# Multiplying the experts' low-rank factors on four partition groups, from a DRAM copy laid out for it

## The chip, the cores and the metric

The kernel runs on one core of one Trainium2 chip. The core has a matrix engine (TensorE, PE in the profile), a vector engine (VectorE, DVE), a scalar engine (ScalarE, ACT), GpSimd (POOL) and SyncE (SP), which in this kernel issues most of the transfers between DRAM and the on-chip memory SBUF. Matmuls write to PSUM, from where DVE or ACT read. The engines run side by side, each its own instructions in order, and wait for each other by semaphores. The metric is the time of one execution on the device in microseconds (us); several executions are made and the median is given. One further execution is recorded by the hardware profiler, and the trace and the profile page come from that one.

## The reference

Two transformer layers over `x` of 4 x 1024 tokens with 256 features, all in fp32. Layer 0 is causal attention and a feed-forward block beside each other, layer 1 is gated group attention and a mixture of eight experts of which each token uses two. What the change touches are the weights of the experts: each is a dense matrix and a product of two low-rank factors (rank 16).

```python
# layer 0
xn = layernorm(x)
x = x + attention0(xn) + relu(xn @ W1 + b1) @ W2 + b2
# layer 1, experts (E = 8, D = 256, HID = 512, R = 16)
def _lora_in(xf, W, b, A, B):                   # W [E, HID, D], A [E, R, D], B [E, HID, R]
    base = einsum('td,ehd->teh', xf, W)
    low = einsum('ter,ehr->teh', einsum('td,erd->ter', xf, A), B)
    return base + low + b
...
h1 = _lora_in(xf, W1, b1, A1, B1)
h3 = _lora_in(xf, W3, b3, A3, B3)
g = silu(h1) * h3
y_e = _lora_out(g, W2, b2, A2, B2)              # the same with HID and D exchanged
y = einsum('te,ted->td', gates, y_e)            # gates: top 2 of 8, normalised
```

Since `base + low` is `xf` times (W + A B), the kernel adds the products A B to the dense weights once, and uses the sum for all tokens.

## The kernel before

Layer 0 is a loop over 16 **units** `u` of 256 tokens: batch `b = u // 4`, quarter `p = u % 4`. The tokens' rows stay in SBUF (`xs`). The source gives each unit's steps in a fixed sequence, interleaved with steps of its neighbours; within that, the framework's scheduler puts the instructions of each engine into an order when the program is built, by what it estimates to be ready, and from then on each engine's order is fixed. In unit `u` stand, in the source:

- `turns` (L549 to L557): the attention weights of unit `u` are transposed on PE (`pt`, L554) and copied to `attT`, for half 0 by ACT, for half 1 by DVE (L556).
- `hidden` (L534 to L546): the feed-forward block, PE L541 and ReLU on ACT L544.
- `first_turn(u + 2)`: a normalised unit is transposed, from unit 3 on by a DVE transpose of a strip read back from DRAM (L457).
- `merge(u, qTs[u])`: the loads for the merging of expert weights; described below.
- `queries(u + 1)`, then `norms_turn(u - 1)` (L632 to L646): the layer-1 input `xl` of the unit before is transposed on PE (L638) and copied by ACT.
- `weighted(u)` (L560 to L580): attention weights times values. For units with `p > 0` from unit 2 on, distant weights come back from DRAM as two bands, which DVE transposes (L568) into `attT`; PE L573 and L576; DVE forms `zT`.
- `logits(u - 1)` (PE L655), `scores(u + 1)`, the second half of `hidden`, statistics of a later unit.
- `finish(u)` (L584 to L606): PE `po` (L592) and `pv` (L596); ACT squares `pv` and forms `rs` (L601, L190, L191); DVE adds into `x` (L598, L605) and takes statistics (L184 and L185).
- `multiply()`: the products that `merge` returned (in the last unit ahead of `finish`).
- `norms(u)` (L609 to L631): from the statistics a chain DVE, ACT (logarithm and exponential at L190 and L191), DVE (L615, L616), ACT again, DVE (L618, L620), then `xl` (L623, two instructions), ACT `xr` (L627).

The merging shares 8 experts out over the 16 units: unit `u` does half `c = u % 2` of expert `e = u // 2`. With `c == 0` the expert's six factors, one packed row of 3 x 768 for each rank, are loaded by three transfers to `lt` [96, 768] at partitions 0, 32 and 64, 16 partitions each (L400). One buffer serves for `lt`, so the loads for the next expert wait for the last multiplication from it. Each unit loads 768 KB of dense weights to `wt` (L405). `multiply` makes three products of 128 x 512 in PSUM, the third from two matmuls, adds each to `wt` on DVE (L419), and stores the sums to the DRAM tensors `wm13` and `wm2` (L420, L422), which the expert stage of layer 1 reads.

`second` (L334 to L358) is called at unit 0 and puts layer 1's weights and constants on SP's queue: `raw`, `rowt`, `wvl_s`, `wg_s`, `wo_s`, `rope_s`, then zeros to `yg`, `posb_s`, and the bias columns and rows of the experts (`cols`, eight of `eb2`). The loads of the first `merge` follow on the same queue. A DMA of SP is issued under one of eight semaphores in turn, and waits for the transfer that used it last.

Of the kernel before, what the change touches and what calls it, by code (L numbers as in the profile page):

```python
# [9 lines left out]
F32 = mybir.dt.float32  # L10
AF = mybir.ActivationFunctionType
ALU = mybir.AluOpType
# [5 lines left out]
P = 128  # L18
B, N, D = 4, 1024, 256
NT = N // P  # L20
DC = D // P
# [4 lines left out]
E, HID, R = 8, 512, 16  # L26
# [21 lines left out]
EB2, W2B = EC * D, EC * D + D  # L48

LN_ = D + HID  # L50

# [14 lines left out]
def block_kernel(ctx: ExitStack, tc: tile.TileContext, x, wq, wk, wv, wfc, w1, w2, wqk, wvl, wg,  # L68
                 wo, wr, ew, el, eb2, cols, rows, rope, posb, out):
    nc = tc.nc  # L70
# [15 lines left out]
    def load_x(b, p, n=1, after=None):  # L86
        tt = slice(2 * p, 2 * (p + n))
        w = nc.sync.dma_start(out=xs[b][:, tt, :], in_=x[b].rearrange("(t p) d -> p t d", p=P)[:, tt, :])
        if after is not None:
            tc.add_manual_dep(w.ins, after.name, landed, reason="what is needed first goes first")  # L90
# [80 lines left out]
    dram = ctx.enter_context(tc.tile_pool(name="dram", bufs=1, space=DRAM))  # L171
# [5 lines left out]
    atd = dram.tile([B * NP, 2 * P, (NP - 1) * 2 * P], F32, name="atd")  # L177

    rd = [dram.tile([N, 4 * QK], F32, name=f"rd{b}") for b in range(B)]
    xld = [dram.tile([P, DC, N], F32, name=f"xld{b}") for b in range(B)]  # L180

    def stats(src, mv, t, tag="st"):
# [57 lines left out]
    with ExitStack() as l0:  # L240
        wp = l0.enter_context(tc.tile_pool(name="l0w", bufs=1))
        p_sc = l0.enter_context(tc.tile_pool(name="p_sc", bufs=2, space=PSUM))
# [8 lines left out]
        act = l0.enter_context(tc.tile_pool(name="l0a", bufs=2))  # L251
# [84 lines left out]
        def second(after):  # L336
            def load(eng, **k):
                tc.add_manual_dep(eng.dma_start(**k).ins, after.name, landed, reason="what is needed first goes first")

            load_x(1, 0, NP, after)  # L340
            raw = wp.tile([P, DC, QK], F32, name="raw")
            load(nc.sync, out=raw, in_=wqk)
            load(nc.sync, out=wqr_s[:, :, QK:], in_=wr)
            load(nc.sync, out=rowt, in_=rows[RE:].partition_broadcast(P))
            load(nc.sync, out=wvl_s, in_=wvl)
            load(nc.sync, out=wg_s, in_=wg)
            load(nc.sync, out=wo_s, in_=wo)
            load(nc.sync, out=rope_s, in_=rope)

            load(nc.sync, out=yg[NF * TB + NSURE * HB :, :].rearrange("(k p) d -> p k d", p=P),  # L350
                 in_=zero.unsqueeze(1).to_broadcast([P, (NHB - NSURE) * HB // P, D]))

            nc.gpsimd.memset(posb_s, FAR)
            for g in range(P // G):
                load(nc.sync, out=posb_s[ts(g, G), ts(g, G)], in_=posb)
            for name, at in (("eb1", EB1), ("eb3", EB3)):
                nb = COLS[name][0]
                load(nc.sync, out=wm13[:, :, at : at + EC].rearrange("e p m -> p e m"),  # L358
                     in_=cols[:, nb : nb + E * EC].rearrange("p (e m) -> p e m", e=E))
            for e in range(E):  # L360
                load(nc.sync, out=wm2[e, :, EB2:], in_=eb2[e].partition_broadcast(P))
            return raw
# [32 lines left out]
        def merge(u, after):  # L395
            e, c = u // DC, u % DC
            if c == 0:
                lt = act.tile([96, LN_], F32, tag="lt", name="lt", bufs=1)
                for k in range(3):
                    w = nc.sync.dma_start(out=lt[32 * k : 32 * k + R, :], in_=el[e][:, k * LN_ : (k + 1) * LN_])  # L400
                    tc.add_manual_dep(w.ins, after.name, landed, reason="what is needed first goes first")
                merge.lt = lt
            lt = merge.lt
            wt = act.tile([P, 3, HID], F32, tag="wt", name="wt")
            w = nc.sync.dma_start(out=wt, in_=ew[e].rearrange("p (k c w) -> p k c w", k=3, c=DC)[:, :, c, :])  # L405
            tc.add_manual_dep(w.ins, after.name, landed, reason="what is needed first goes first")
            f1, f3, f2 = lt[0:R, :], lt[32 : 32 + R, :], lt[64 : 64 + R, :]

            def multiply():

                pab, pc = (p_sc.tile([P, 2, HID], F32, tag="sc", name=n) for n in ("pab", "pc"))
                pa, pb, pc = pab[:, 0], pab[:, 1], pc[:, 0].rearrange("p (i d) -> p i d", i=2)
                nc.tensor.matmul(pa, f1[:, ts(c, P)], f1[:, D : D + HID], start=True, stop=True)
                nc.tensor.matmul(pb, f3[:, ts(c, P)], f3[:, D : D + HID], start=True, stop=True)
                for i in range(2):
                    nc.tensor.matmul(pc[:, i, :], f2[:, ts(2 * c + i, P)], f2[:, HID : HID + D],
                                     start=True, stop=True)
                for k, p in enumerate((pa, pb, pc.rearrange("p i d -> p (i d)"))):
                    nc.vector.tensor_tensor(wt[:, k, :], p, wt[:, k, :], ALU.add)  # L419
                nc.sync.dma_start(  # L420
                    out=wm13[e, :, 0:EB1].rearrange("p (k c w) -> p k c w", k=2, c=DC)[:, :, c, :], in_=wt[:, 0:2, :])
                nc.sync.dma_start(out=wm2[e, :, ts(c, HID)], in_=wt[:, 2, :])  # L422
            return multiply
# [310 lines left out]
        for u in range(U):  # L734
            b, p = divmod(u, NP)
# [4 lines left out]
            if u == 0:  # L740
                raw = second(qTs[0])
# [16 lines left out]
            if u == 0:  # L758
                fuse_values()
            multiply = merge(u, qTs[u])  # L760
            if u + 1 < U:
                qT = queries(u + 1)
# [677 lines left out]
```

## Time and profile before

| what | value |
|---|---|
| median of 3 runs | 1122.03 us (1120.65 to 1123.66) |
| profiled execution | 1116.86 us |
| its span, first to last instruction | 1115.2 us |
| mean granted TensorE clock | 0.997 |
| PE busy from 110 to 115 us, and from 115 to 120 us | 5.00 and 5.00 us |
| DVE busy in the same stretches | 1.47 and 4.21 us |
| adds of the merge, L419, 128x512, `pab` / `pc` | 0.666 / 0.678 us each |
| load of dense weights, L405, 16 times 768 KB | 6.0 us to landing |
| load of factors, L400, 48 KB each, the first three | 4.5 us to landing |

The profiled execution lies below all three timed runs; what is worked out from its rows is worth what it is against its own time. In rows of the trace, the first number is the start in us from the span's start, the second is the busy time of the row, which may hold several instructions (x8). "L413" is the line, then come the operation, the output and the inputs by their names in the program, and their sizes. A bracket at the end gives the idle time of the engine ahead of the row and what ended it. PE is the matmul, PEld the load of its weights, SPq the issuing of transfers on SP. An fp32 matmul leaves two records for its two passes.

### The profile page before, as it was taken

Reading aid. Unit: us, or ns where it says so; the run is one execution under the profiler, and the core shown is the slowest. Engines: PE = TensorE matmul, PEld = TensorE weight load, DVE = VectorE, ACT = ScalarE, POOL = GpSimd, SP = SyncE. Lnnn points to the kernel's source line nnn. Section 1 sums busy time; section 2 is a strip of 40 time slices with the busy share of each in tenths; the row PEclk is TensorE's granted clock in tenths of the full one; section 3 lists DMA queues with packets and bytes.
Section 4 is the critical chain, followed back from the end, with each engine's and each line's share of the span. In section 5 each row is a group of like instructions: output and inputs, shape, how many; then the busy total and the mean of one; then the engine's idle time right before and its main releaser. Section 6 shows DMA issues by size and latency. Waiting matters only on the chain. (4 is left out here: it accounts for less than half of the span.)

```text
span 1115.2 us, 15338 instructions
## 1 busy us (share of the span) xinstructions
PE 1099.2 (99%) x5084; PEld 861.1 (77%) x5084; DVE 557.0 (50%) x1536; ACT 285.4 (26%) x755; POOL 173.8 (16%) x216
## 2 busy tenths in 40 slices
PE   8999999999999999999999999999999999999997
PEld 6788888888888888874588888888888885555645
DVE  5434464445544355456674554454332323384956
ACT  3323333234333232224201111111111112112021
POOL 2200001222131113332000000000000003362410
PEclk9999999999999999999999999999999999999999
DMA  8735434564454335521547887787877764353211
GB/s 311 202 101 155 136 100 132 162 190 118 118 175 131 116 101 165 162 109 43 183 118 239 272 266 223 211 285 218 258 233 233 232 173 103 94 138 90 81 42 39
DMA packets 211953, 180.06 MB, mean 161 GB/s; under 512 B 135968, under 2 KB 181536, under 8 KB 206752
## 3 DMA queue, kind: packets, MB, share of 16 engines
q1 hardware_dynamic: 121200, 141.03, 40.0%
q10 hardware_dynamic: 84528, 21.25, 8.4%
q0 software_dynamic: 6144, 16.79, 4.6%
q8 instruction: 41, 0.67, 0.3%
q14 instruction: 40, 0.33, 0.1%
HBM read 125.93 MB, written 54.17 MB: 161 GB/s over the span
## 5 line engine op out<-in xcount | busy, mean ns | idle before, releaser
L959 PE MATMUL p<-xT,w 128*128 128x256 f32 (+1 forms) x1152 | 241.2, 368 | 0.0
L959 PEld LDWEIGHTS p<-xT,w 128*128 128x128 f32 x1152 | 209.4, 190 | 26.9 <-issue 0.3
L964 ACT ACTIVATE s<-p,w 128x256 f32<-128x256 f32 (+1 forms) x144 | 58.8, 459 | 313.9 <-PE p L959 210.4
L1044 POOL DMA_INDIRECT y<-yg,slot x64 | 61.7, 964 | 487.4 <-DVE v L1169 420.4
L968 DVE SCALAR_TENSOR_TENSOR g<-p,w,s 128x256 f32<-128x256 f32 (+1 forms) x144 | 61.0, 462 | 137.3 <-PE p L959 131.4
L981 PE MATMUL py<-w,g 128*128 128x256 f32 x544 | 123.4, 379 | 0.0
L541 PE MATMUL pm<-xnT,w_s 128*128 128x256 f32 x512 | 118.5, 379 | 0.0
L592 PE MATMUL po<-w_s,hT 128*128 128x256 f32 x512 | 116.1, 380 | 0.0
L981 PEld LDWEIGHTS py<-w,g 128*128 128x128 f32 x544 | 102.9, 190 | 14.1 <-DVE g L968 0.3
L592 PEld LDWEIGHTS po<-w_s,hT 128*128 128x128 f32 x512 | 96.9, 190 | 20.1 <-issue 8.0
L541 PEld LDWEIGHTS pm<-xnT,w_s 128*128 128x128 f32 x512 | 95.6, 192 | 11.6
L716 POOL DMA_INDIRECT xg<-xr,put x64 | 63.7, 995 | 209.2 <-ACT hT L544 138.8
L494 PE MATMUL sc<-xnT,qT 128*128 128x256 f32 (+1 forms) x320 | 65.8, 361 | 0.0
L544 ACT ACTIVATE hT<-pm,colt 128x256 f32<-128x256 f32 x128 | 53.9, 466 | 42.3 <-PE pm L541 42.2
L596 PE MATMUL pv<-vo_s,zT 128*128 128x512 f32 x128 | 60.1, 592 | 0.0
L1167 PE MATMUL pv<-wvl_s,xl 128*128 128x512 f32 x128 | 57.7, 597 | 1.6 <-DVE v L1169 1.5
L494 PEld LDWEIGHTS sc<-xnT,qT 128*128 128x128 f32 x320 | 54.6, 191 | 6.0 <-ACT qT L481 0.2
L1243 PE MATMUL pg<-xl,wg_s 128*128 128x512 f32 x128 | 58.3, 595 | 0.0
L1290 PE MATMUL pj<-wo_s,gd 128*128 128x256 f32 x256 | 56.7, 380 | 0.6 <-DVE o L1292 0.4
L1290 PEld LDWEIGHTS pj<-wo_s,gd 128*128 128x128 f32 x256 | 48.1, 190 | 7.9 <-DVE o L1292 0.9
L605 DVE SCALAR_TENSOR_TENSOR x<-pv,rs,x 128x256 f32<-128x256 f32 x32 | 15.5, 484 | 72.4 <-ACT rs L191 57.1
L983 DVE TENSOR_TENSOR yt<-py,w 128x512 f32<-128x512 f32 (+1 forms) x36 | 23.8, 660 | 51.1 <-PE py L981 51.1
(261 smaller groups left out, 1330.2 us busy)
## 6 DMA issues: line engine op xcount, KB each, us to landing
w<-wm SPq DMA_DIRECT2D x36, 1028.0 KB, 7.4
w<-wm SPq DMA_DIRECT2D x36, 640.0 KB, 4.7
wt<-in_ew_dram SPq DMA_DIRECT2D x16, 768.0 KB, 6.0
wm<-wt SPq DMA_DIRECT2D x16, 512.0 KB, 2.8
xt<-xg ACTq DMA_DIRECT2D x128, 64.0 KB, 4.3
yg<-yt ACTq DMA_DIRECT2D x32, 256.0 KB, 5.2
xnd<-xn SPq DMA_DIRECT2D x16, 256.0 KB, 3.3
wm<-wt SPq DMA_DIRECT2D x16, 256.0 KB, 2.9
```

What stands on the lines that cost most here:

```text
L494: nc.tensor.matmul(sc[:, kp * 2 * P : kp * 2 * P + w], qT[:, c, ts(i, P)], xnTs[b * NP + kp][:, c, 0:w], start=(c == 0), stop=(c == DC - 1))
L541: nc.tensor.matmul(pm[:, j, :], w1_s[:, c, ts(2 * m2 + j, P)], xnTs[u][:, c, :], start=(c == 0), stop=(c == DC - 1))
L592: nc.tensor.matmul(po[:, i, :], hT[:, m, ts(i, P)], w2_s[:, m, :], start=(m == 0), stop=(m == IC - 1))
L596: nc.tensor.matmul(pv, zT[:, c, ts(i, P)], vo_s[:, c, :, :], start=(c == 0), stop=(c == DC - 1))
L716: w = nc.gpsimd.indirect_dma_start(out=xg, out_offset=bass.IndirectOffsetOnAxis(ap=put[:, b * NT + t : b * NT + t + 1], axis=0), in_=xrs[b ...
L959: nc.tensor.matmul(p[:, j, :], w13[:, w0 : w0 + P], xT[:, c, :], start=(c == 0), stop=(c == DC - 1))
L964: up.silu = nc.scalar.activation(s[:, j, :], p1[:, j, :], AF.Silu, bias=w13[:, EB1 + m : EB1 + m + 1]).ins
L968: up.g = nc.vector.scalar_tensor_tensor(g[:, m, :], p3[:, j, :], w13[:, EB3 + m : EB3 + m + 1], s[:, j, :], ALU.add, ALU.mult).ins
L981: down.last = nc.tensor.matmul(py[:, k, :], g[:, m, ts(k, P)], w2[:, m * D : (m + 1) * D], start=(m == 0), stop=(m == EC - 1)).ins
L1044: w = nc.gpsimd.indirect_dma_start(out=ys[b][:, t, k, :], out_offset=None, in_=yg, in_offset=bass.IndirectOffsetOnAxis(ap=slot[:, n : n + ...
L1243: gate_sum.last = nc.tensor.matmul(pg, wg_s[:, c, ts(m, P)], a.xl[:, c, ts(h, T * P)], start=(c == 0), stop=(c == DC - 1)).ins
L1290: nc.tensor.matmul(pj, a.gd[:, m, ts(n, P)], wo_s[:, m, :], start=(m == 0), stop=(m == HC - 1))
```

## The change

The factors of all experts are first copied, within DRAM, to a tile `eld` of 4 groups x 128 rows (8 experts x 16 ranks) x 896 columns. Ten DMAs on SP's queue do that (five for each `k`), placed in `second` behind `rope_s` and ahead of `yg`; one of each five has pieces of 128 numbers (512 bytes). Together they write 1.57 MB.

`lt` becomes [128, 896], loaded from `eld` by four transfers at partitions 0, 32, 64 and 96 (16 x 640 for groups 0 and 1, 16 x 896 for groups 2 and 3). Groups 0 and 1 hold the first factors of `W1` and `W3` with 384 of the 512 columns (`CUT`) of the second. Groups 2 and 3 hold each a half of the factors of `W2` (256 columns of output), and beside them the first factor of `W1` or `W3` again with the last 128 columns of the second. So each group streams 384 columns in a unit. `multiply` has six matmuls instead of four, and still three adds, of 768, 512 and 256 columns (two of them on two separate stretches) instead of three times 512.

When the program is built, the scheduler orders instructions anew. On PE the merge stays where it was, behind `finish`, save that in the last unit another part of it is placed ahead of L638. On DVE, in units 1 to 13, the order from L605 on was `x`, statistics L184, add, L185, add, add, L615, L616, L618, L620, copy of `attT`, `xl`, both band transposes. It becomes `x`, add (768), L184, add (512), L185, add (256), L615, L616, copy of `attT`, L618, L620, and then, in units 1, 2, 6 and 10, one band transpose, `xl`, and the other; in unit 3 the transpose of a strip, `xl`. In unit 0 the adds come behind the first of the two `xl`. On ACT a ReLU of `hidden` is placed between the second logarithm and exponential of `norms`. On SP the ten copies stand where the source has them, and the four loads of `lt` directly behind the loads of `eb2`. The order in layer 1 is unchanged.

```diff
+CUT = HID - P
...
+    eld = dram.tile([4, E * R, 3 * D + P], F32, name="eld")
...
             load(nc.sync, out=rope_s, in_=rope)
+
+            rows_el = el.rearrange("e r n -> (e r) n")
+            for k in range(2):
+                a0 = k * LN_
+                load(nc.sync, out=eld[k, :, 0 : D + CUT], in_=rows_el[:, a0 : a0 + D + CUT])
+                load(nc.sync, out=eld[2 + k, :, 0:D].rearrange("r (c p) -> r c p", c=DC),
+                     in_=rows_el[:, 2 * LN_ : 2 * LN_ + HID].rearrange("r (c i p) -> i r c p", c=DC, i=2)[k])
+                load(nc.sync, out=eld[2 + k, :, D : 2 * D], in_=rows_el[:, 2 * LN_ + HID :])
+                load(nc.sync, out=eld[2 + k, :, 2 * D : 3 * D], in_=rows_el[:, a0 : a0 + D])
+                load(nc.sync, out=eld[2 + k, :, 3 * D :], in_=rows_el[:, a0 + D + CUT : a0 + LN_])
...
-                lt = act.tile([96, LN_], F32, tag="lt", name="lt", bufs=1)
-                for k in range(3):
-                    w = nc.sync.dma_start(out=lt[32 * k : 32 * k + R, :], in_=el[e][:, k * LN_ : (k + 1) * LN_])
+                lt = act.tile([P, 3 * D + P], F32, tag="lt", name="lt", bufs=1)
+                for k in range(4):
+                    n = D + CUT if k < 2 else 3 * D + P
+                    w = nc.sync.dma_start(out=lt[32 * k : 32 * k + R, 0:n], in_=eld[k, e * R : (e + 1) * R, 0:n])
...
-            f1, f3, f2 = lt[0:R, :], lt[32 : 32 + R, :], lt[64 : 64 + R, :]
+            f = [lt[32 * k : 32 * k + R, :] for k in range(4)]
             def multiply():
-                pab, pc = (p_sc.tile([P, 2, HID], F32, tag="sc", name=n) for n in ("pab", "pc"))
-                pa, pb, pc = pab[:, 0], pab[:, 1], pc[:, 0].rearrange("p (i d) -> p i d", i=2)
-                nc.tensor.matmul(pa, f1[:, ts(c, P)], f1[:, D : D + HID], start=True, stop=True)
-                nc.tensor.matmul(pb, f3[:, ts(c, P)], f3[:, D : D + HID], start=True, stop=True)
+                pab, pcd = (p_sc.tile([P, 2, HID], F32, tag="sc", name=n) for n in ("pab", "pcd"))
+                for k in range(2):
+                    nc.tensor.matmul(pab[:, k, 0:CUT], f[k][:, ts(c, P)], f[k][:, D : D + CUT], start=True, stop=True)
                 for i in range(2):
-                    nc.tensor.matmul(pc[:, i, :], f2[:, ts(2 * c + i, P)], f2[:, HID : HID + D],
+                    nc.tensor.matmul(pcd[:, i, 0:D], f[2 + i][:, ts(c, P)], f[2 + i][:, D : 2 * D],
                                      start=True, stop=True)
-                for k, p in enumerate((pa, pb, pc.rearrange("p i d -> p (i d)"))):
-                    nc.vector.tensor_tensor(wt[:, k, :], p, wt[:, k, :], ALU.add)
+                for k in range(2):
+                    nc.tensor.matmul(pcd[:, k, D:CUT], f[2 + k][:, 2 * D + c * P : 2 * D + (c + 1) * P],
+                                     f[2 + k][:, 3 * D :], start=True, stop=True)
+                w2 = wt[:, 2, :].rearrange("p (i d) -> p i d", i=2)
+                for out, more in ((wt[:, 0:2, 0:CUT], pab[:, :, 0:CUT]), (w2, pcd[:, :, 0:D]),
+                                  (wt[:, 0:2, CUT:], pcd[:, :, D:CUT])):
+                    nc.vector.tensor_tensor(out, more, out, ALU.add)
```

## The prediction

> **What bounds the kernel now.** I read the page from its first row, then the engines' busy time in stretches, then single rows around one merge.
>
> ```profile
> span 1115.2 us, 15338 instructions
> PE 1099.2 (99%) x5084; PEld 861.1 (77%) x5084; DVE 557.0 (50%) x1536; ACT 285.4 (26%) x755; POOL 173.8 (16%) x216
> ```
>
> TensorE has records on it 99% of the time, VectorE half. Cut into 5 us pieces, the stretch from 25 to about 475 us (where layer 0 ends) has PE busy 5.00 of 5.00 in each piece I asked for. So layer 0, which holds all that changes, is PE's: an edit counts as far as it shortens PE's queue or makes PE wait. Of unit 2 (rows of PE and DVE, others left out):
>
> ```profile
> 113.95 0.69 PE L413 MATMUL pab<-lt 16*128 16x512 f32 x1
> 113.95 0.69 PE L414 MATMUL pab<-lt 16*128 16x512 f32 x1
> 113.96 0.69 PE L416 MATMUL pc<-lt 16*128 16x256 f32 x2
> ...
> 114.48 0.59 PE L413 MATMUL pab<-lt 16*128 16x512 f32 x1
> ...
> 115.02 0.33 PE L554 MATMUL pt<-ident,att 128*128 128x128 f32 x1
> ...
> 115.13 0.48 DVE L605 SCALAR_TENSOR_TENSOR x<-pv,rs,x 128x256 f32<-128x256 f32 x1 [2.36 <-PE pc L416]
> 115.99 0.67 DVE L419 TENSOR_TENSOR wt<-pab,wt 128x512 f32<-128x512 f32 x1
> 116.58 0.17 DVE L185 BATCH_NORM_AGGREGATE mean<-st 128x2 f32<-128x6 f32 x1
> 119.26 0.73 DVE L623 TENSOR_SCALAR xl<-x,mean,rstd 128x256 f32<-128x256 f32 x2
> 119.90 1.83 DVE L568 STREAM_TRANSPOSE attT<-band 128x768 f32<-128x768 f32 x2
> ...
> 120.59 0.60 PE L638 MATMUL pt<-ident,xl 128*128 128x128 f32 x4
> ```
>
> Two things are to be seen. The three row groups start within 0.01 us of each other and the whole group takes 115.02 - 113.95 = **1.07 us**: that is all the merge costs PE. And PE turns `xl` (L638) only shortly after DVE made it: the first `xl` ends near 119.67, PE takes it at 120.59 (0.92 later); the second ends at 119.99, the third transpose comes near 120.80 (**0.81** later). In units 2 to 14 these two margins are nearly constant. That is the wait that is nearest.
>
> **Part 1: four groups instead of three (PE).** Each fp32 matmul shows as two passes. From 113.95 to 114.48 is a load and one 512-column pass, 0.53 us; a pass by itself is the 0.427 us by which a 512-column stream advances, the load 0.107; after the second pass 0.10 goes by before the next 128-row tile. Old sum: 0.107 + 2 x 0.427 + 0.10 = 1.06 (row: 1.07). New: groups 0 and 1 have 384 columns, 0.320 a pass: 0.107 + 0.640 + 0.10 = 0.85; groups 2 and 3 have 256 + 128 columns, the same. Saved 0.21 a unit, 16 units: **-3.4 us**. Should the four groups' loads not hide (one-column matmuls of L376, 16 in 1.84 us, give 0.115 for a load), 0.1 a unit is left, -1.6.
>
> A rule speaks for that lower figure, since groups 2 and 3 now run two matmuls each, of which the second is short. In the first merge, taken row by row, L416's four passes start at 46.81, 47.13, 47.34 and 47.55: the first step holds the load (0.107 + 0.213), the next two are 0.21, which is just 256 columns at 0.83 ns, so a second matmul in a group cost its columns and nothing on top. The Trainium skill (TensorEngine Tiling (Array Packing), section "Instruction Overhead") puts an overhead of about 60 cycles on every matmul. At a cycle a column that is 0.05 us a pass; the two extra passes would lengthen groups 2 and 3 to 0.95, and save 0.11 a unit, 1.8 us in all, against 3.4 by the row. I take the row; its second matmul had 256 columns and the new one has 128, so 1.8 stays as an end.
>
> **Part 2: VectorE.** The adds still move 1536 columns: 3 x 0.67 = 2.01 us before. A 256-column add from PSUM takes 0.425 (L598), a 512 one 0.67, so 768 is an estimate of 0.92; 0.92 + 0.67 + 0.43 = 2.02. The sum is nothing, the **order** is not. The scheduler now puts the 768-wide add ahead of the BN statistics and the 512-wide add ahead of L185. Back-to-back DVE rows start 0.08 before the row ahead ends. From 115.13: add at 115.53, statistics 116.37, second add 116.72, L185 at 117.31 instead of 116.58: 0.73 late. Before, 0.48 of that was waiting anyway (Exp L191 ended at 117.33, L615 stood behind the third add until 117.84): 0.25 is left. A ReLU (0.46) now stands on ACT between the second Ln and Exp; it costs 0.22 net of the overlap. The `attT` copy (0.42, between L620 and `xl`) moves ahead into the wait, -0.34. So `xl` is later by about 0.15, plus whatever now stands between L620 and `xl`, which differs:
>
> - Units 2, 6, 10: a 768-wide band transpose, 0.95 - 0.08: `xl` is 1.02 late. PE comes 0.21 earlier. Margin 0.81 - 0.21 = 0.60, stall 0.42, net **+0.21** each, 0.6.
> - Unit 3: a strip transpose (0.71): 0.78 late. Here the next unit has no bands, so PE's L655 follows at once and waits for ACT's copy of the turned `xl`; in such a unit of before that copy ends at 271.58 and L655 starts at 271.63. With 0.05 of margin the lateness comes through: **+0.7**. Units 7 and 11 have nothing in between: 0.15 each, 0.3.
> - Unit 1: its margin at L638 is 3.7 us, but a strip transpose now stands ahead of the second band transpose, which L576 waits for: +0.4 of 0.63.
> - Units 4, 8, 12: about 0.5 late, within the margin: -0.2 saved, half of it lost at `zT`: -0.1 each, -0.3. Units 5, 9, 13: 0.5 to 0.7 late, +0.1 each, +0.3. Units 0, 14, 15: nothing.
>
> Sum 0.6 + 0.7 + 0.3 + 0.4 - 0.3 + 0.3 = **+2.0** in place of -3.4. Its bounds: -3.4 if DVE's order is covered, +3.6 if each banded unit also loses 0.1 to 0.2 at L576.
>
> **Part 3: ten transfers and a detour (SP's queue).**
>
> ```profile
> 28.67 7.45 SPq L338 DMA_DIRECT2D wm<-in_eb_dram  x8
> 36.23 1.44 SPq L400 DMA_DIRECT2D lt<-in_el_dram  x3
> 37.77 0.61 SPq L405 DMA_DIRECT2D wt<-in_ew_dram  x1
> ...
> 46.80 0.69 PE L413 MATMUL pab<-lt 16*128 16x512 f32 x1
> ```
>
> SP issues in order, and each issue waits until the transfer eight before it has landed; that paces the eight `eb2` transfers at 0.93 us, the last of them at 0.66. The last of `lt` is issued at about 36.8 and lands after 4.2, at 41.4: PE, which wants it at 46.80, has 5.4 us to spare. The change puts ten transfers (1.57 MB) into the queue behind `rope`, ahead of all these rows, and a fourth `lt` (0.5). They have no row in this trace. Below: their bytes at the 400 GB/s of 20 to 28 us, 3.9 us. Above: ten at the first `eb2` pace, 9.3. I take 10 x 0.66 = 6.6, since the queue and not the bytes sets the pace after 28 us. Then `lt` lands at 41.4 + 0.5 + 6.6 = 48.5: PE waits **+1.8** (0 to 4.6 by the ends). The first `wt` lands near 51.5 instead of 44.5, but its adds now stand behind the first `xl` on DVE; the second `xl`, `rowt` and `bg_s` queue behind them: up to +1. The strips behind them have slack (their turn is needed near 61). Later `lt` loads have a unit or more. Such a gap can also cost clock:
>
> ```profile
> 24.00:26.00 2.00, 2.00 (x6) 1.58 (x5) 2.00 (x10) 0.62 (x3) 0.17 (x1) 0.50 1.01 408
> ```
>
> (columns: sum, PE, PEld, DVE, ACT, POOL, then clock, DMA share, GB/s). After PE had been busy only 1.39 of 2.00 in 20 to 22 us and 0.65 before, the clock fell to 0.73 and then 0.50. After a short gap I take no dip; with one like this, 3.4 us at half clock, +1.7.
>
> Layer 1's instructions keep their order and PE is busy there throughout, so layer 0's end passes through one to one. Sum: +2.0 + 1.8 = 3.8, about **+4**. On the profiled execution 1116.86 us (span 1115.2 and 1.7 around it) that is 1121; the median of the runs shown is 1122.03, 5 above, so I forecast **1126**.
>
> **Rivals.**
>
> *Faster: everything hides.* If DVE's shifts stay within the margins and `lt` comes in time (bytes, not queue, set the pace), only part 1 remains: -3.4, 1118.6. For it: DVE is half idle. Against it: margins of 0.05 and 0.81 in the rows. Chance 0.10.
>
> *Half hides: no change.* The late `lt` costs 1.8, the order of DVE costs just what PE gains in banded units, the rest saves 3.2: -1.4, 1120.6. For it: shifts of 0.5 are inside the margin. Chance 0.20.
>
> *Worse: the start breaks.* `lt` at its upper end, the wait decides from 5.4 us of delay on: 3.5 stall, 1.7 clock, and 3.6 from the units: +8.8, 1130.8. For it: PE did lose the clock at 24 us. Against it: the queue is nearly empty from 31 to 33 us. Chance 0.15.
>
> *The change does not do what it says:* the loads or the short passes don't hide and PE's group shrinks by 0.1 instead of 0.21; this adds 1.6 to the forecast (1127.6) and stays inside the range.
>
> **Numbers.** Forecast +4: 0.55 (own range +1.5 to +7). Range: 1119 (half of the fastest case left out) to 1131. A difference under 0.3%, 3.4 us, can't be told from none in this kernel: faster is below 1118.7, slower above 1125.4. Faster: most of the first rival, 0.08. Slower: the fourth case and 0.45 of the forecast's 0.55, 0.60. Same: 0.32.
>
> **What would show it.** Step 1: the merge group lasts 0.85 us, all four groups starting together. Step 2: PE idle before L638's successor, released by DVE `xl`, 0.2 to 0.6 us in units 2, 6, 10, and before the logits by an ACT copy in unit 3; L185's row 0.7 later than now after the merge. Step 3: PE idle 0 to 4 us before the first merge, released by a DMA into `lt`, near 47 us. Wrong if PE has no idle at the turn of `xl`, or if `lt` lands before 46.8.

## The result, and the profile after

The changed kernel is slower: 1130.67 us against 1122.08 us, medians of 11 runs each (1127.75 to 1135.79 against 1120.65 to 1125.48), a ratio of 1.0079 with a 95% interval of 1.0065 to 1.0092. The forecast was 1126, slower by about 4, in a range of 1119 to 1131.

The page of the changed kernel begins:

```profile
span 1126.9 us, 15478 instructions
PE 1099.9 (98%) x5148; PEld 861.3 (76%) x5148; DVE 559.2 (50%) x1536; ACT 287.1 (25%) x755; POOL 172.9 (15%) x216
```

PE's busy time has not fallen (1099.2 before), although its matmuls for the merge are shorter: a row under a lower clock lasts longer, and here the clock was at 0.50 from 22 to 28 us (before: 0.73, 0.50 and 0.91 in the same three stretches of 2 us). What is lost is seen in rows. In the changed kernel all lines from the merge on stand 18 lower, so L605 is now L623, L185 L187, L623 L641, L638 L656. These are the rows of PE and DVE for the merge of unit 2 and what follows it:

```profile
117.61 0.59 PE L427 MATMUL pab<-lt 16*128 16x384 f32 x2
117.63 0.70 PE L429 MATMUL pcd<-lt 16*128 16x256 f32 x4
...
118.16 0.39 PE L432 MATMUL pcd<-lt 16*128 16x128 f32 x4
...
118.48 0.33 PE L572 MATMUL pt<-ident,att 128*128 128x128 f32 x1
...
118.79 0.48 DVE L623 SCALAR_TENSOR_TENSOR x<-pv,rs,x 128x256 f32<-128x256 f32 x1 [2.36 <-ACT rs L193]
...
119.19 0.95 DVE L437 TENSOR_TENSOR wt<-pab,wt 128x768 f32<-128x768 f32 x1
...
120.98 0.17 DVE L187 BATCH_NORM_AGGREGATE mean<-st 128x2 f32<-128x6 f32 x1
...
123.10 0.98 DVE L586 STREAM_TRANSPOSE attT<-band 128x768 f32<-128x768 f32 x1
124.00 0.69 DVE L641 TENSOR_SCALAR xl<-x,mean,rstd 128x256 f32<-128x256 f32 x2
...
124.52 0.67 PE L656 MATMUL pt<-ident,xl 128*128 128x128 f32 x4 [0.31 <-DVE xl L641]
```

PE's group takes 118.48 - 117.61 = 0.87 us instead of 1.07. On DVE the aggregate comes 2.19 us after L623 began (before: 1.45), `xl` 5.21 after it (before: 4.13). PE, which had 0.92 us to spare, now waits 0.31 for it.

The start, in the rows of SP's queue and of PE:

```profile
23.54 9.90 SPq L340 DMA_DIRECT2D eld<-in_el_dram  x10
...
36.90 7.14 SPq L340 DMA_DIRECT2D wm<-in_eb_dram  x8
44.52 1.77 SPq L413 DMA_DIRECT2D lt<-eld  x4
...
49.44 0.67 PE L427 MATMUL pab<-lt 16*128 16x384 f32 x2 [1.24 <-DMA lt<-eld]
```

The ten copies hold SP for 9.90 us, `lt` is issued at 44.52 instead of 36.23, and PE waits for it. PE itself also comes to this merge 1.4 us later than before (it is free for it at 48.20), after the longer stretch at half clock.

To see where the time went, each PE instruction of a run was put beside the same one of the kernel before, and the distance of their starts taken at the merges. A number that grows is time lost between two rows; one that stays is none. All in us, against the first profile of the kernel before.

| PE start at | before, again | changed | changed, again | e1 | e2 | e3 | e4 | e5 | e6 | e7 | e8 | e9 | e10 |
|---|---|---|---|---|---|---|---|---|---|---|---|---|---|
| merge of unit 0 | -0.73 | 2.64 | 1.36 | 5.43 | 2.34 | 1.23 | 5.82 | -0.02 | 0.04 | -0.94 | 0.01 | -0.16 | 1.66 |
| merge of unit 1 | -0.73 | 3.20 | 1.91 | 5.23 | 10.24 | 3.76 | 5.62 | -0.02 | -0.17 | -1.14 | -0.20 | -0.16 | 2.20 |
| merge of unit 14 | -0.72 | 6.00 | 4.59 | 7.64 | 10.92 | 2.82 | 4.12 | 0.10 | -1.13 | 0.97 | -3.86 | -1.16 | 0.93 |
| experts begin (573) | 0.11 | 6.39 | 6.16 | 9.30 | 11.24 | 2.30 | 3.74 | -0.47 | -1.61 | 0.92 | -4.89 | -2.42 | 0.39 |
| last matmul | 5.45 | 11.85 | 12.16 | 9.32 | 11.24 | 2.30 | 3.76 | 4.88 | 4.27 | 7.05 | 1.12 | 3.86 | 6.76 |

The last row needs a word. The changed kernel's two profiles and seven others lose 5.3 to 6.4 us between 985 and 1006 us, in layer 1, where PE stands still for 3.2 to 4.8 us in one to three gaps. This is PE's row at the first of them in the changed kernel, and then in the second profile of the kernel before:

```profile
998.75 1.99 PE L1308 MATMUL pj<-wo_s,gd 128*128 128x256 f32 x8 [2.93 <-issue]
```

```profile
992.38 1.99 PE L1290 MATMUL pj<-wo_s,gd 128*128 128x256 f32 x8 [2.88 <-issue]
```

So the kernel before has it too. It is missing in its first profile and in e1 to e4. Those four ran on chip 12, where the kernel before takes 1116.96 us. The other eight repeats and experiments, on chips 10, 13 and 15, all have it, and there the kernel before takes 1121.9 to 1122.8. It goes with the chip, then, and not with the change. It is also as large as the 5 us by which the first profile (1116.86) lay below the timed runs; on which chip that profile was taken is not recorded. What stops PE there is not shown. The change costs the profiled execution 6.4 us, then, all of it in layer 0.

### The profile page after: what moved, and what is told of

The parts are those of the page before. It is cut to its first block, busy times and chain, and to the rows that moved or that the text cites. A ratio compares the mean times of both kernels' runs of the same rounds, so it can differ in the third digit from the quotient of the medians.

```text
span 1126.9 us, 15478 instructions
## 1 busy us (share of the span) xinstructions
PE 1099.9 (98%) x5148; PEld 861.3 (76%) x5148; DVE 559.2 (50%) x1536; ACT 287.1 (25%) x755; POOL 172.9 (15%) x216
## 5 line engine op out<-in xcount | busy, mean ns | idle before, releaser
L623 DVE SCALAR_TENSOR_TENSOR x<-pv,rs,x 128x256 f32<-128x256 f32 x32 | 15.5, 484 | 73.7 <-ACT rs L193 66.9
```

## The experiments

Ratios are against runs of the kernel before on the same chip, with 95% intervals. The expectations of e1 to e4 name times against 1122 us; on their chip the kernel before takes 1117, so there the ratio is what can be compared.

**The changed kernel and the kernel before, again.** Nothing edited.

> The changed kernel once more, for a second profile of it, on the same chip as the runs beside it. In its first profile layer 0 ended 6.4 us late and layer 1 lost another 5.3 us between 994 and 1002 us, where PE, VectorE and GpSimd stood still together with no releaser shown. If that belongs to the kernel, it is there again; if it was a passing event, layer 1 is shifted by a constant. Units 1 to 13 lose 2.8 us again, within 0.1; the start may differ with the clock.

> The kernel before, unedited, for a second profile. On one chip five profiles (the changed kernel twice, three edits) lost 5.3 to 6.1 us together between 990 and 1002 us in layer 1, on the other chip, whose times of the kernel before are 5 us lower, none of four did. If this belongs to the chip and not to the change, this profile shows it too where the time of the kernel before is near 1122, and does not where it is near 1117. If it belongs to the change, it is never here.

1130.18 us against 1122.77, 1.0075 (1.0059 to 1.0091). From unit 1 to unit 14 it loses 2.7 us (2.8 in the first profile), unit by unit the same to 0.1. The start and the end of layer 0 differ. The wait at the first merge is gone:

```profile
48.16 0.59 PE L427 MATMUL pab<-lt 16*128 16x384 f32 x2
```

PE was ready for it at the same time as in the first profile (48.2), but `lt` was issued 0.75 us sooner. The kernel before, again: 0.9997 (0.9988 to 1.0006). Against the first one its merges stand at a constant -0.73, so that differences of 0.1 between merges mean something.

**e1: the copies on another queue.** All ten are edited like the first:

```diff
-                load(nc.sync, out=eld[k, :, 0 : D + CUT], in_=rows_el[:, a0 : a0 + D + CUT])
+                load(nc.gpsimd, out=eld[k, :, 0 : D + CUT], in_=rows_el[:, a0 : a0 + D + CUT])
...
```

> The changed kernel with its ten DRAM copies issued by GpSimd instead of SyncE; nothing else is edited. Queue theory (the copies cost time because SyncE issues in order and each waits for the transfer eight before it): the first lt lands near 42 to 43 us, PE does not wait at the first merge (1.24 us before it now), layer 0 ends about 1.3 to 2 us earlier than in the changed kernel, and the time falls to about 1129. Bytes theory (the 1.57 MB themselves hold up what is behind them): lt still lands 3 us or more later than in the kernel before, PE still waits about 1 us, and nothing is won. Both leave the 3.1 us that units 1 to 15 lost.

1124.79 us, 1.0073 (1.0058 to 1.0088): nothing won that can be told. PE does not wait at the first merge, as the queue theory had it. But it is 5.4 us late when it gets there. GpSimd issued the copies from 14.3 us on, 9 us sooner than SP could, just behind SP's issue of the last part of `x` (14.26), which DVE needs next:

```profile
28.07 0.75 DVE L186 BATCH_NORM_STATS2 st<-x 128x6 f32<-128x256 f32 x2 [6.54 <-DMA x<-in_x_dram]
```

These rows of `x` landed at 28.04, 13.8 us after their issue; in the kernel before they took 9.5 (13.69 to 23.16). The DMA engines are full in this stretch (share 1.0 or more from 14 to 30 us). At the 400 GB/s that they move there, 1.57 MB take 3.9 us, an estimate that covers most of the 4.3 us of delay. So neither theory came true as it was put: `lt` is in time, and the bytes cost as much at another place. The edit moved the cost and did not remove it.

**e2: the copies alone.** The ten copies in the kernel before; three groups, `lt` straight from `el`.

> The kernel before with only the ten DRAM copies added on SyncE's queue at the same place; three row groups, lt straight from el. Queue theory: the third lt lands near 41.4 + 8 = 49 us, PE waits 1 to 2 us before the first merge, and from there the distance to the kernel before stays constant to the end of layer 0: +1 to +3 us in all, about 1124. Rival (the copies are harmless, all of the loss is in the units): no wait at 47 us, within 0.5 us of the kernel before.

1120.25 us against 1116.96, 1.0032 (1.0021 to 1.0044). The wait comes with no other part of the change:

```profile
49.13 1.19 PE L425 MATMUL pab<-lt 16*128 16x512 f32 x1 [3.41 <-DMA lt<-in_el_dram]
```

It is longer than in the changed kernel, since here PE had kept its clock from 18 to 30 us and came to the merge sooner. What followed in this execution is in the stretches after it (sum, PE, PEld, DVE, ACT, POOL, clock, DMA share, GB/s):

```profile
50.00:55.00 5.00, 5.00 (x15) 2.75 (x11) 2.16 (x6) 0.47 (x1) 0.00 (x0) 0.50 0.90 314
55.00:60.00 5.00, 5.00 (x22) 4.34 (x21) 0.98 (x4) 2.14 (x6) 0.00 (x0) 0.50 0.83 238
60.00:65.00 5.00, 5.00 (x15) 4.06 (x15) 1.35 (x5) 2.46 (x6) 1.27 (x1) 0.50 0.27 66
65.00:70.00 5.00, 5.00 (x27) 4.40 (x26) 0.77 (x2) 1.91 (x4) 0.00 (x0) 1.00 0.00 0
```

After a gap of 3.41 us the clock stood at half for 15 us, and the distance went from 2.34 to 10.24. From there it grows by 0.7 more up to unit 14, in units 1 and 3, where constant was expected. The median of the timed runs (3.3 above) says that most executions pay only the wait; the profiled one was the slowest of the ten (1118.93 to 1127.98).

**e3: DVE's order put back.** `issue_after` sets an order on an engine and adds no wait: the first add behind L184's instruction, the other two behind L185's, and in `weighted` the band transposes behind `xl`.

```diff
-                    nc.vector.tensor_tensor(out, more, out, ALU.add)
+                    with tc.issue_after(at):
+                        nc.vector.tensor_tensor(out, more, out, ALU.add)
...
-                with tc.issue_after(turns.copy):
+                with tc.issue_after(turns.copy), tc.issue_after(norms.xl):
```

> The changed kernel with four groups and copies on SyncE as it is, but VectorE's order put back by edges: first add behind L184, the other two behind L185, the band transposes behind xl. Order theory: L185 comes only 0.25 us later than before, the stalls at the turn of xl go, and units 1 to 15 win 0.2 us each instead of losing 3.1 in all: from the first merge to the end of layer 0 about 3 us shorter than the kernel before (2 to 3.2), 6 us shorter than the changed kernel; with the start's +2.9 the time is near that of the kernel before, 1121.5 to 1123. Rival (the six short matmuls or the four groups themselves slow PE down): no change against the changed kernel, 1130.

1117.52 us, 1.0007 (1.0000 to 1.0015): of the changed kernel's 0.8% it takes back nearly all. From unit 1 to 14 it gains 0.94 us where the changed kernel lost 2.80. So the order was the cause of the units' loss, and the four groups do not slow PE. But the gain is a third of what was expected. `xl` comes as long after the merge's `x` as before (4.14 us, before 4.13), no sooner. Units 4, 5, 8, 9, 12 and 13 keep their 0.2. In 2, 6 and 10 the bands, which ended 0.06 us ahead of PE before, and in 3, 7 and 11 the logits with their 0.05 had no margin to give: there the 0.2 becomes a wait.

**e4: both edits.**

> Both edits: copies on GpSimd and VectorE's order put back. If both theories hold the costs add: no wait at the first merge, every unit 0.2 us shorter, layer 0 ends 2 to 3 us before the kernel before, time about 1119 (1118 to 1121). If the bytes hold up the loads, about 1122; if the order is not the cause, 1127 to 1129.

1121.1 us, 1.0036 (1.0023 to 1.0049), slower than with the order alone: it has the start of e1 (5.8) and, from unit 1 to 14, a gain like e3's (-1.5). The expected time, 3 us below the kernel before, assumed that another queue costs nothing.

**e7: expert 0 straight from `el`.** For expert 0 the layout is made by ten small transfers into `lt`, two for groups 0 and 1 and eight for groups 2 and 3, cut like the DRAM copies, and the ten DRAM copies are issued in unit 1.

```diff
+                for k in range(2 if e == 0 else 0):
+                    part(k, lambda t: t[:, 0 : D + CUT], el[0][:, a0 : a0 + D + CUT])
...
-                for k in range(4):
+                for k in range(4 if e else 0):
```

> The changed kernel with its own VectorE order, but expert 0's factors loaded straight from el by ten small transfers (six more than now), and the ten DRAM copies issued in unit 1 instead. Queue theory: the last lt lands near 41.4 + 7 x 0.55 = 45.3 us, PE does not wait at the first merge (1.24 us in the changed kernel) and no clock dip follows; from the first merge on the same losses as in the changed kernel (+2.8 to 3.2): 1.0035 to 1.005 of the kernel before. Rival (the start's loss is the clock's chance only): as slow as the changed kernel.

1126.42 us, 1.0039 (1.0026 to 1.0052). PE reaches the first merge without a wait. Against the changed kernel on the same chip (1130.18) half of the loss is gone, most of it by taking the copies out of the start. Not all: from unit 1 to 14 it loses 2.1 us instead of 2.8, because in unit 3, which loses 0.2 instead of 0.78, the scheduler now leaves the strip's transpose behind `xl`.

**e6: that, and e3's order.**

> The same start as in the run with expert 0 loaded directly, and VectorE's order put back as in the third experiment. Both theories: no wait at the first merge, then -0.2 us in about half of the units: layer 0 ends 1 to 2 us before the kernel before, 0.998 to 1.0 of its time. If the copies cost elsewhere (bands and strips behind them in unit 1), up to 1.002.

1122.07 us, 0.9994 (0.9986 to 1.0002); layer 0 ends 1.6 us early, as expected. Both losses are gone, and what is left of the gain can't be told from nothing.

**e8: the adds behind the bands.** As e6, with the three adds called in `weighted` after the band transposes of the next unit; `norms.xl` is there the last band transpose, or the second `xl` where there is none.

```diff
+            if u:
+                with tc.issue_after(norms.xl):
+                    merge.adds()
```

> As the run before this one in the list, but all three adds of the merge stand behind xl and the band transposes of the next unit on VectorE. If only VectorE's order ahead of xl decides, xl now comes about 1 us earlier than in the kernel before, and each of 15 units keeps the whole 0.2 us: -3 us at the end of layer 0, 0.9965 to 0.998. Rival (the adds then hold up zT, or the PSUM that scores needs): PE waits at zT's reader or at the scores, 1.0 or more.

1118.99 us against 1122.77, **0.9963** (0.9950 to 0.9975): faster than both kernels. These are its rows of DVE and PE behind the merge of unit 2, which began at 113.55:

```profile
115.71 0.18 DVE L188 BATCH_NORM_AGGREGATE mean<-st 128x2 f32<-128x6 f32 x1
...
117.64 0.73 DVE L664 TENSOR_SCALAR xl<-x,mean,rstd 128x256 f32<-128x256 f32 x2
...
119.98 0.60 PE L679 MATMUL pt<-ident,xl 128*128 128x128 f32 x4
...
120.38 0.92 DVE L456 TENSOR_TENSOR wt<-pab,wt 128x768 f32<-128x768 f32 x1
```

`xl` begins 4.09 us after the merge began (before: 5.31, changed: 6.39) and PE takes it 1.9 us after it is there (before: 0.92). The adds begin 6.8 us after the merge, and PE shows no wait in units 0 to 13. Each unit keeps 0.2 us, and units 2, 3, 6, 7, 10 and 11 gain 0.32 to 0.42. The 0.1 to 0.2 on top are of the order alone, since e9 gains them in the same units with three groups. With -4.9 at the end of layer 0, more was won than the expected 3.

**e9: late adds with the old maths.** Three groups, own loads, adds behind the bands.

> The kernel before, three groups, with all adds behind xl and the band transposes, as in the fastest run. It tells what the four groups are worth there: order theory, with the groups worth 0.2 us in 15 or 16 units: layer 0 ends 1.5 to 2 us before the kernel before (4.9 less 3.2), 0.998 to 0.999. If the order alone makes the gain, it is as fast as that run, 0.9963.

1120.54 us, 0.9982 (0.9976 to 0.9989). Layer 0 ends 2.4 us early by the order alone (1.5 to 2 was expected). Between unit 1 and 14 it gains 1.0, e8 3.66: the four groups are worth 2.7 us in 13 units, 0.20 each, once nothing stands in their way.

**e5: the new order with the old maths.** First add ahead of L184, second ahead of L185, three groups.

> The kernel before, three groups and its own loads, with only VectorE's order turned: first add of the merge ahead of L184, second ahead of L185 (the scheduler then puts band transposes ahead of xl as well). Order theory: xl 1 us or more later, PE idles at its turn in units 2, 6, 10 and at the logits in 3, 7, 11; without the 0.2 us that the four groups save, each such unit loses 0.2 more than in the changed kernel: +4 to +6 us by the end of layer 0, 1.0035 to 1.0055. Rival (the loss needs the shorter PE group, which makes PE arrive early): below +2 us.

Missed: 0.9998 (0.9990 to 1.0006), and 0.12 us lost from unit 1 to 14 instead of 4 to 6. The rows of unit 2 say why; its merge began at 113.93:

```profile
117.03 0.17 DVE L188 BATCH_NORM_AGGREGATE mean<-st 128x2 f32<-128x6 f32 x1
...
120.30 0.69 DVE L634 TENSOR_SCALAR xl<-x,mean,rstd 128x256 f32<-128x256 f32 x2
...
120.82 0.67 PE L649 MATMUL pt<-ident,xl 128*128 128x128 f32 x4
```

With adds of 512 the aggregate is 0.47 late, not 0.74, and that is about the 0.48 us of waiting that followed anyway; `xl` is still 1.0 late in this unit because a band is turned ahead of it, PE starts 0.25 late, and about half of that is made up by the next merge. PE also comes 0.21 us later to `xl` than with four groups, so the rival has its part in it. That adds stand ahead of the statistics is, then, not enough. It takes how late `xl` comes in each unit.

**e10: the same three adds, in another sequence.**

```diff
-                for out, more in ((wt[:, 0:2, 0:CUT], pab[:, :, 0:CUT]), (w2, pcd[:, :, 0:D]),
-                                  (wt[:, 0:2, CUT:], pcd[:, :, D:CUT])):
+                for out, more in ((wt[:, 0:2, CUT:], pcd[:, :, D:CUT]), (w2, pcd[:, :, 0:D]),
+                                  (wt[:, 0:2, 0:CUT], pab[:, :, 0:CUT])):
```

> The changed kernel with one edit: its three adds stand in the source as 256, 512, 768 columns. The scheduler then puts them on VectorE as add (768) ahead of L184, add (256) ahead of L185, add (512) behind it, and no band or strip transpose ahead of xl any more; the copies stay on SyncE. Size theory (what decides is how late xl comes, not that adds stand ahead of the statistics): L185 is 0.48 us late instead of 0.73, xl no more than 0.1 us late, so units 2 to 13 keep 0.1 to 0.2 us each instead of losing: from unit 1's merge to unit 14's -1 to -2.5 us (+2.8 in the changed kernel). The start keeps its loss of 1 to 4 us: 1.000 to 1.003 of the kernel before. Rival (any add ahead of the statistics costs as much): +2 us or more over those units, 1.006.

1123.4 us against 1121.9, 1.0012 (0.9999 to 1.0025). From unit 1 to 14 it gains 1.27 us where the changed kernel loses 2.80, with the 768-wide add still ahead of the statistics. In unit 2, where L623 begins at 117.64:

```profile
119.56 0.17 DVE L187 BATCH_NORM_AGGREGATE mean<-st 128x2 f32<-128x6 f32 x1
...
121.48 0.74 DVE L641 TENSOR_SCALAR xl<-x,mean,rstd 128x256 f32<-128x256 f32 x2
```

The aggregate is 0.47 late (1.92 after L623, before 1.45), as in e5, but no band stands ahead of `xl`, which comes 0.29 early (3.84, before 4.13). A shuffle of three source lines is worth 4 us of layer 0, through what the scheduler makes of it. The gain is spent at the start, on the copies: the ratio can't be told from none.

## Why the prediction was right, and where it was too small

The direction was right and each of the three parts names what the rows show. The size was not: 8.6 us against 4, and that 1130.67 lies inside the range, by 0.3 us, is luck, as several terms were too small together.

**Part 1 holds.** Forecast 0.85 for the group, measured 0.866; the second matmul of a group starts when the columns of the first are through, with nothing on top (passes at 0.33, 0.55 and 0.66 us after the group's start). The overhead of 60 cycles a matmul (the Trainium skill, TensorEngine Tiling (Array Packing), "Instruction Overhead"), which the prediction turned into 0.95, is not in these rows. The four groups are worth 0.2 us a unit, as e8 against e9 shows, and the -3.4 exists. It was not to be had with this order.

**Part 2 holds step by step.** The add of 768 was estimated at 0.92 and took 0.95; L185 0.73 late, measured 0.74; `xl` 1.02 late in unit 2, measured 1.08. By unit (from its merge to the next):

| unit | 1 | 2 | 3 | 4 | 5 | 6 | 7 | 8 | 9 | 10 | 11 | 12 | 13 | sum |
|---|---|---|---|---|---|---|---|---|---|---|---|---|---|---|
| forecast | 0.4 | 0.2 | 0.7 | -0.1 | 0.1 | 0.2 | 0.15 | -0.1 | 0.1 | 0.2 | 0.15 | -0.1 | 0.1 | 2.0 |
| measured | 0.46 | 0.18 | 0.78 | -0.20 | 0.21 | 0.38 | 0.20 | -0.21 | 0.20 | 0.38 | 0.20 | -0.19 | 0.41 | 2.8 |

The wait that was named for unit 3 is there, in the rows of ACT and PE:

```profile
156.19 0.60 ACT L661 COPY xl<-pt 128x512 f32<-128x512 f32 x1
...
156.85 1.11 PE L673 MATMUL pl<-wqr_s,xl 128*128 128x72 f32 x8 [0.56 <-ACT xl L661]
```

What was mis-sized is the term for the units that turn bands: 5, 6, 9 and 10 lose about twice their share, 13 four times. In 6 and 10 PE waits 0.52 us for `xl`, where 0.42 was forecast, and in 13 0.23; in 5 and 9 it waits at the bands. Unit 1 came out by luck: the margin of 3.7 us is that of unit 0's `xl` (turned at 57.82), while unit 1's own had 0.92, like the others, and PE loses 0.2 there.

Units 0, 14 and 15, put at nothing, cost 0.56 and 0.39. In unit 0 the four parts of `lt` landed one by one in the first profile and stretched the group to 1.35 us. In the second it took 0.87, and unit 0 lost the same 0.55, by a wait that the prediction does not have. PE needs a copy of attention weights, which ACT makes behind the scaling of layer 1's weights:

```profile
55.77 0.66 PE L572 MATMUL pt<-ident,att 128*128 128x128 f32 x4 [0.53 <-ACT attT L574]
```

In unit 15 PE waits 1.41 us for unit 14's `xl`, where it waited 0.79 before: the margin of 0.9 us that was said to hold up to unit 14 is missing there.

**Part 3 had the mechanism, and the wrong size.** "10 x 0.66 = 6.6" was 9.90, above even the upper end of 9.3. The 0.66 was read from issues that wait for nothing. Of the ten copies the fourth to the seventh waited for loads ahead of them in the queue: in e2, whose trace has the landings, three of them are issued 0.02 us after the transfer eight before has landed (25.36, 26.65, 27.92). Part of the delay came back in the queue behind, so that `lt` was issued 8.3 us later. The wait forecast was 1.8 (by its own figures 1.7, and 4.4 at the upper end, not 4.6 or 3.5). It was 1.24 and 0 in the two profiles of the changed kernel, 1.06 in e3 and 3.41 in e2. It depends on when `lt` is issued (43.42 to 45.35 us in these four) and on when PE is ready: 45.7 in e2, which kept its clock from 18 to 30 us, 48.2 in both of the changed kernel, which had 0.50 from 22 to 28. Both differ from execution to execution without any edit; whether the change has a part in that clock is not shown. "After a short gap I take no dip" was the second half of the error: e2 and e3 show dips behind this wait.

The sum in the profiled execution is 2.64 at the first merge, 0.56 in unit 0, 2.80 in units 1 to 13 and 0.39 after, together 6.4. By the timed runs the copies alone cost 3.6 (e2's 0.32% of 1122) and the units 3.2 (2.8 + 0.4), together 6.8 of 8.6. The cost of the copies is not one number: the changed kernel against e7 gives 3.8, or 3.2 without unit 3; e3 against e6, on two chips, 1.5.

The remaining 2 us lie between executions. The profiled one took 1128.57 us, 2.1 below the median of its kernel. Of the five runs above the median four had a mean granted clock of 0.988 to 0.992, against 0.996 in the profiled one; the fifth had 0.997. In e7 the profiled run (1123.89, clock 0.997) is the fastest, and the other four (1126.1 to 1128.2) had 0.993 or 0.994. Where clock can go is seen in unit 15. Behind the wait of 1.4 us the first profile of the changed kernel, then its second (columns as above):

```profile
485.00:490.00 5.00, 3.81 (x21) 3.43 (x22) 2.25 (x4) 1.82 (x5) 4.20 (x5) 1.00 0.38 138
```

```profile
485.00:490.00 5.00, 5.00 (x19) 4.24 (x18) 0.83 (x1) 1.41 (x4) 4.02 (x4) 0.66 0.37 136
```

The second lost 1.57 us in units 14 and 15 instead of 0.39; e1, with the same wait and a dip, lost 1.66, and e7, without a dip, nothing more than the first. No profile has a dip behind the waits of 0.1 to 0.6 us in units 1 to 13, so how the rest of the 2 us comes about stays open.

The rival that lay nearest on the worse side, a broken start at +8.8, gives the measured time, but not by its own account: it put 3.6 into the units and 5.2 into one wait with its dip (by its own figures 6.1).

## What to carry to other kernels

When one engine is the bound, a change that shortens its own work also brings it sooner to whatever it waits for next; look up that margin first, and follow what a scheduler does with the instructions ahead of it. Work for which nobody waits belongs behind the chain for which somebody does, and to say so by an edge alone (e9, 2.4 us of layer 0) was worth more here than the shorter matmuls without it (e6, 1.6). A table prepared once in DRAM should not stand in the queue ahead of its first user; load the first piece directly.

## What the runs showed of the hardware

- Row groups of 16 partitions run side by side in fp32: four groups of 384 columns each, in two passes, take 0.866 us up to the start of the next product, three groups of 512 take 1.07.
- DRAM to DRAM copies of 64 to 320 KB were issued 0.99 us apart on SP (ten in 9.90), four of them after waiting for the transfer eight before; the `eb2` loads of 128 KB behind them 0.89 apart (eight in 7.14).
- A gap of 3.41 us on PE was followed by half the clock for 15 us, and the next merge came 7.9 us later than it would have; gaps of 1.06 (e3) and 1.40 us (the changed kernel, again) by a mean clock of 0.68 and 0.66 over 5 us, gaps of 1.24 and 1.41 us (the changed kernel) by no dip.
- On chips 10, 13 and 15 PE stands still for 3.2 to 4.8 us in layer 1, at a cost of 5.3 to 6.4 us, in each of eight profiles and in the changed kernel's first, whose chip is not recorded; on chip 12 in none of four, whatever the edit.
